# Series of extra matmuls behind the last output: a conv kernel on one core

## The chip, the cores and the metric

The kernel runs on one core of a Trainium2 chip. The metric is the device time of one execution in microseconds (us). Two runs of the kernel before gave 2524.60 and 2525.92 us, a median of 2525.26.

## The reference

An image batch `x` of shape (4, 32, 32, 16) passes through four layers, each added to its input after a group normalisation. Layers 0, 1 and 3 are of one kind, a convolution whose 3 x 3 kernel differs for each of the 1024 output positions; layer 2 works on intervals (running maxima and two small dynamic-programming steps).

```
first   = einsum('ijyx,byxc->bijc', M, inputs)
shifted = conv(inputs, G as h*w*f kernels of 3x3xC)      # for every position (i,j) an own kernel
diff    = relu(inputs[:, None, None] - shifted)
second  = einsum('ijyx,bijyxc->bijc', W, diff)
return first - second
...
x = x + conv0(_gn(x)); x = x + conv1(_gn(x)); x = x + interval2(_gn(x)); x = x + conv3(_gn(x))
```

The heavy part is `shifted`: 1024 positions x 16 filters as output rows, 144 taps and channels as the contraction, and 1024 image positions for each of 4 images as columns, in three layers. The result wanted is the final `x`.

## The kernel before

The batch is cut into two groups of two images (`NG = 2`, `GB = 2`). Three conv layers of two groups each make six phases. A phase has eight chunks (`NT`) of 128 output positions, and a chunk has 32 steps, one for each filter and image: 6 x 8 x 32 = 1536 steps.

A step computes a [128 x 1024] block: for 128 output positions, the convolution with one filter over one image, into a pair of PSUM banks (`bank_pair`, four pairs in rotation, which is all of PSUM). The upper and lower halves of the image (512 columns each) go to the two banks of the pair. The contraction is laid on 64 partitions at a time, and the array is used as two row tiles: `products` (line 601 has its matmul) issues for each of its operand pairs one matmul on partitions 0 to 63 and one on 64 to 127, which run side by side, each into its own bank. I call such two matmuls a pair. In steps with split operands there are seven pairs:

- `first_part`: two with weights `WU` and columns `iy`, two with `WL` and `iz`; then ScalarE scales the whole block in place (line 630);
- `second_part`: two with `WD` and `iyz`, one with `W9` and `im9` (the ninth tap). In this last pair one of the two matmuls has only `LAST` = 480 columns instead of `NH` = 512; which tile that is changes with the image `b`. Then VectorE takes the minimum with zero, multiplies with the weights `WT` and sums (line 646).

The operands are F32R except in the first 16 steps, which use plain f32. All is written for one `manual_schedule`: instructions stand on each engine in the order of the Python code. `conv_layer` issues the first part of a step before the second part of the step ahead of it, so that TensorE works on one step while ScalarE scales another. Preparation of weights (`prep_parts`), normalisation, the interval layer and the `first` terms are generators that are advanced between the steps. `wpool` holds the prepared weights: `parts` (both row tiles' `WU`, `WL`, `WD` for four filters) and `W9`, for a unit of four filters at a time.

At the end, the last step's second part is issued, VectorE reduces the last block and adds it to `X[1]`, and SP sends the last chunk of `X[1]` to `out`. The end of the kernel waits for all engines' queues and for the DMAs.

Of the kernel before, what the change touches and what calls it, by code (L numbers as in the profile page):

```python
# [15 lines left out]
P = 128  # L16
B, H, C = 4, 32, 16
NG = 2
GB = B // NG
# [8 lines left out]
NH = HI * H  # L28
# [3 lines left out]
FU = 4  # L32
NU = C // FU
# [9 lines left out]
def net_kernel(ctx: ExitStack, tc: tile.TileContext, x, xq, xi, convs, iv_w, iv_b, out):  # L43
# [26 lines left out]
    nc = tc.nc  # L70
# [13 lines left out]
    def bank(name):  # L84
        return bank_pair(name)[:, 0]
# [3 lines left out]
    n_chunks = len(phases) * NT  # L89
# [12 lines left out]
    raws, units, chunks = {}, {}, {}  # L102

    def load_raw(u):
        if u < n_chunks * NU:
            n = u // NU
            raws[u] = wpool.tile([P, 3, FU, P], F32, tag="raw", bufs=RAWS, name=f"raw_{u}")
            nc.sync.dma_start(raws[u], convs[phases[n // NT][1]][2][n % NT, u % NU])
# [13 lines left out]
    iy = [const.tile([P, 2, GB, NH], F32R, name=f"iy{g}") for g in range(NG)]  # L122
    iz = [const.tile([P, 2, GB, NH], F32R, name=f"iz{g}") for g in range(NG)]
    iyz = [const.tile([P, 2, GB, NH], F32R, name=f"iyz{g}") for g in range(NG)]
    im9 = [const.tile([P, GB, NH], F32R, name=f"im9{g}") for g in range(NG)]
# [45 lines left out]
    def halve(dst, src, mask):  # L171
        nc.scalar.activation(dst, src, AF.Copy, scale=mask[:, 1:2])  # L172
# [19 lines left out]
    def upper(src, n, name):  # L192

        t = work.tile([P, 2, NH], F32, tag="upper", bufs=2, name=f"upper_{name}")[:, :n]
        t = t.rearrange("p s (y x) -> p s y x", x=src.shape[3])
        nc.vector.tensor_scalar(  # L196
            t.bitcast(I32), src.bitcast(I32), HIGH, None, op0=ALU.bitwise_and
        )
        return t.rearrange("p s y x -> p s (y x)")

    def prep(u, at=0, to=FU, eng=nc.gpsimd):

        if u >= n_chunks * NU:
            return
        f0 = u % NU * FU
        for s in range(2 if u < PLAIN else 1):
            eng.tensor_tensor(  # L207
                raws[u][:, s, at:to], raws[u][:, s, at:to],
                pick[s][:, f0 + at : f0 + to].unsqueeze(2).to_broadcast([P, to - at, P]),
                ALU.subtract,  # L210
            )

    def prep_parts():

        for u in range(PLAIN, n_chunks * NU):
            parts = wpool.tile([P, 2, 3, FU, P], F32R, tag="parts", bufs=AHEAD + 1, name=f"parts_{u}")
            W9 = wpool.tile([P, FU, P], F32R, tag="W9", bufs=AHEAD + 1, name=f"W9_{u}")  # L220
            units[u] = [parts[:, :, k] for k in range(3)] + [W9]
            src = raws.pop(u)
            w8 = src[:, 0].rearrange("p f k -> p (f k)")
            WU, WL, WD = (parts[:, 0, k].rearrange("p f k -> p (f k)") for k in range(3))
            high = upper(src[:, 0:1], 1, f"w{u}")[:, 0]
            yield (IDLE,)
            halve(W9, src[:, 1], low_w)
            yield ()
            nc.scalar.activation(WD, high, AF.Copy, scale=-EPS)  # L229
            nc.gpsimd.tensor_tensor(WL, w8, high, ALU.subtract)  # L230
            nc.gpsimd.tensor_tensor(W9, W9.bitcast(F32), src[:, 2], ALU.add)  # L231
            yield ()
            nc.scalar.copy(WU, high)  # L233
            nc.gpsimd.tensor_tensor(WD, WD.bitcast(F32), WL.bitcast(F32), ALU.add)  # L234
            yield ()
            prep(u + 1)
            yield (IDLE,)
            yield (IDLE, CALM)
            for h in range(2):
                nc.sync.dma_start(  # L240
                    parts[64 * h : 64 * h + 64, 1].bitcast(F32),
                    parts[64 - 64 * h : 128 - 64 * h, 0].bitcast(F32),
                )
            load_raw(u + RAWS)
            yield (IDLE, CALM)
            yield (IDLE, CALM)
# [477 lines left out]
    pairs = const.tile([P, C // 2], F32, name="pairs")  # L724
# [17 lines left out]
    rows = const.tile([P, 2, 4], F32, name="rows")  # L742
# [23 lines left out]
    def first_stats(src, name):  # L766

        ps = bank(f"ps_{name}")
        by_batch = work.tile([P, GB], F32, tag="by_batch", name=f"by_batch_{name}")
        nc.vector.tensor_scalar_mul(by_batch, own, src)  # L770
        nc.tensor.matmul(  # L771
            ps[:, :GB], lhsT=to_rows.rearrange("p k g s -> p (k g s)"), rhs=by_batch,
            start=True, stop=True,
        )
        return ps[:, :GB]

    nc.vector.tensor_reduce(s1, XQ, axis=AX.X, op=ALU.add)
    ps = bank("ps_own")
# [3 lines left out]
    m = first_stats(s1, "m0")  # L782
# [57 lines left out]
    def rest_of_start():  # L840
# [25 lines left out]
        yield from group_norm(0, "c00", xns[0], 4)  # L866

    parts = prep_parts()
    for phase in range(len(phases)):
        conv_layer(phase, behind(phase))  # L870
    second_part(*open_steps.pop(0))
    nc.sync.dma_start(out[1][:, NT - 1], X[1][:, NT - 1])


# [74 lines left out]
```

## Time and profile before

| what | value |
|---|---|
| median of the runs | 2525.26 us |
| the profiled execution's own time | 2525.65 us |
| its span, from the first to the last instruction | 2523.9 us |
| TensorE busy, instructions | 2509.2 us, 21906 matmuls |
| VectorE, ScalarE, GpSimd busy | 2080.3, 1890.2, 1103.6 us |
| granted TensorE clock, mean over the span | 1.000 |
| last pair of matmuls starts | 2519.22 us |
| last reduction on VectorE starts, takes | 2519.71 us, 1.22 us |
| last output DMA issued, median from issue to landing | 2521.19 us, 1.4 us |

A row of the timeline has the start in us from the span's start, the time from the first start to the last end, the engine, the line, the operation, the tile written and those read, the shape, and how many instructions were merged (x4). Matmuls are pipelined: one of 512 columns is listed with 393 ns, but the next starts long before it ends, so distances between starts are what counts. Rows for weight loads (PEld) run beside those for matmuls (PE).

### The profile page before, as it was taken

How to read it: one execution, taken by the hardware profiler on the slowest of the kernel's cores; microseconds unless marked ns; L12 is line 12 of the kernel's file. 1: busy time of each engine (PE TensorE's matmuls, PEld its weight loads, DVE VectorE, ACT ScalarE, POOL GpSimd, SP SyncE). 2: the span in 40 equal slices, each digit the busy share in tenths (PEclk: the TensorE clock that was granted, in tenths of full speed). 3: DMA queues.
4: the chain of work that ended last, by engine and by line, in shares of the span. 5: the costliest groups of instructions: out<-in, count | busy, mean ns of one | idle time of the engine just before them, and what ended most of it. 6: DMA issues, size and time to landing. Idle time of an engine off the chain costs nothing.

```text
span 2523.9 us, 56662 instructions
## 1 busy us (share of the span) xinstructions
PE 2509.2 (99%) x21906; PEld 2186.7 (87%) x21906; DVE 2080.3 (82%) x3621; ACT 1890.2 (75%) x2181; POOL 1103.6 (44%) x990
## 2 busy tenths in 40 slices
PE   8999999999999999999999999999999999999999
PEld 5888888888888888888888889988999898888887
DVE  8888777888777887777788988888888887778877
ACT  3777777787777777777777777787777777777776
POOL 3445333454333335333345555454646344333332
PEclk9999999999999999999999999999999999999999
DMA  5556444464444654444454444554444466354442
GB/s 173 180 151 169 120 135 137 117 168 139 131 139 131 200 163 118 139 131 133 135 143 134 131 119 136 144 159 128 124 135 137 130 170 201 111 143 134 134 135 53
DMA packets 81182, 353.80 MB, mean 140 GB/s; under 512 B 18448, under 2 KB 20368, under 8 KB 80144
## 3 DMA queue, kind: packets, MB, share of 16 engines
q1 hardware_dynamic: 79920, 349.57, 49.2%
q8 instruction: 172, 2.82, 0.5%
q14 instruction: 98, 0.80, 0.1%
q10 hardware_dynamic: 864, 0.58, 0.1%
q0 software_dynamic: 128, 0.02, 0.0%
HBM read 199.19 MB, written 0.98 MB: 79 GB/s over the span
## 4 chain that ended last, share of the span: by engine, by line
PE 99%; ACT 0%; DVE 0%; issue 0%; POOL 0%; DVEq 0%; ACTq 0%; POOLq 0%
PE pc L601 97%; PE pf L398 1%; ACT pc L630 0%; DVE junk L646 0%; PE ps_l L521 0%; PE ps_r L534 0%; ACT L326 0%; ACT L564 0%; DVE raw L817 0%; PE ps_y L585 0%; DVE kept L761 0%; DVE kept L757 0%; PE ps_v L771 0%; DVE raw L825 0%; DVE squares L794 0%
## 5 line engine op out<-in xcount | busy, mean ns | idle before, releaser
L646 DVE SCALAR_TENSOR_TENSOR junk<-pc,WT 128x1024 f32<-128x1024 f32 x1536 | 1879.7, 1224 | 419.0 <-PE pc L601 377.7
L630 ACT ACTIVATE pc<-pc 128x1024 f32<-128x1024 f32 x1520 | 1531.8, 1008 | 599.6 <-PE pc L601 566.5
L601 PE MATMUL pc<-iy,parts 64*128 64x512 f32 x6080 | 988.7, 393 | 0.1
L601 PE MATMUL pc<-iyz,parts 64*128 64x512 f32 x6080 | 971.8, 389 | 1.9 <-ACT pc L630 1.9
L601 PE MATMUL pc<-iz,parts 64*128 64x512 f32 x6080 | 968.3, 387 | 0.0
L601 PEld LDWEIGHTS pc<-iz,parts 64*128 64x128 f32 x6080 | 624.3, 184 | 85.7
L601 PEld LDWEIGHTS pc<-iyz,parts 64*128 64x128 f32 x6080 | 611.9, 184 | 89.1 <-ACT pc L630 5.8
L230 POOL TENSOR_TENSOR parts<-raw,upper_w 128x512 fp32r<-128x512 f32 x190 | 247.3, 1301 | 1008.6 <-PE pc L601 847.4
L601 PEld LDWEIGHTS pc<-iy,parts 64*128 64x128 f32 x6080 | 619.6, 184 | 78.2 <-issue 4.4
L601 PE MATMUL pc<-im,W 64*128 64x480 f32 (+1 forms) x3072 | 623.4, 384 | 0.0
L601 PEld LDWEIGHTS pc<-im,W 64*128 64x128 f32 x3072 | 311.4, 185 | 46.3 <-issue 3.4
L231 POOL TENSOR_TENSOR W<-W,raw 128x512 fp32r<-128x512 f32 x190 | 248.5, 1308 | 1.9 <-ACT W L172 1.6
L234 POOL TENSOR_TENSOR parts<-parts 128x512 fp32r<-128x512 f32 x190 | 247.8, 1304 | 2.7 <-ACT parts L229 2.5
L207 POOL TENSOR_TENSOR raw<-raw,ident 128x512 f32<-128x512 f32 x190 | 201.5, 1061 | 42.8 <-DMA raw<-in_g 34.8
L172 ACT ACTIVATE W<-raw,low_w 128x512 fp32r<-128x512 f32 x190 | 135.9, 715 | 0.1
L646 DVE DVE_READ_ACCUMULATOR junk<-pc,WT 128x1 f32 x1536 | 127.5, 83 | 0.0
L229 ACT ACTIVATE parts<-upper_w 128x512 fp32r<-128x512 f32 x190 | 118.5, 624 | 4.7 <-DVE upper_w L196 4.7
L233 ACT CAST parts<-upper_w 128x512 fp32r<-128x512 f32 x190 | 117.0, 616 | 0.0
L661 POOL TENSOR_SCALAR acc<-acc 128x32 f32<-128x32 f32 x40 | 11.5, 289 | 163.3 <-DVE junk L646 158.9
L196 DVE TENSOR_SCALAR upper_w<-raw 128x512 int32<-128x512 int32 x190 | 82.4, 433 | 0.2
L553 POOL TENSOR_TENSOR tables<-ft_b,rt 128x1089 f32<-128x1089 f32 x16 | 37.6, 2351 | 0.2
L553 POOL TENSOR_TENSOR tables<-ft_a,rt 128x1089 f32<-128x1089 f32 x16 | 37.7, 2355 | 0.0
(138 smaller groups left out, 397.3 us busy)
## 6 DMA issues: line engine op xcount, KB each, us to landing
raw<-in_g SPq DMA_DIRECT2D x190, 768.0 KB, 7.0
parts<-parts SPq DMA_DIRECT2D x380, 384.0 KB, 5.0
WT<-in_w SPq DMA_DIRECT2D x48, 512.0 KB, 4.7
MT<-in_mt SPq DMA_DIRECT2D x6, 2048.0 KB, 13.6
raw<-xs SPq DMA_DIRECT2D x120, 67.8 KB, 2.4
raw<-in_xi SPq DMA_DIRECT2D x3, 271.0 KB, 4.5
raw<-in_xi SPq DMA_DIRECT2D x1, 813.0 KB, 6.8
xs<-xt SPq DMA_DIRECT2D x20, 34.0 KB, 2.0
```

Of the source, the lines that this page charges most:

```text
L172: nc.scalar.activation(dst, src, AF.Copy, scale=mask[:, 1:2])
L196: nc.vector.tensor_scalar(t.bitcast(I32), src.bitcast(I32), HIGH, None, op0=ALU.bitwise_and)
L207: eng.tensor_tensor(raws[u][:, s, at:to], raws[u][:, s, at:to], pick[s][:, f0 + at : f0 + to].unsqueeze(2).to_broadcast([P, to - at, P]), ...
L229: nc.scalar.activation(WD, high, AF.Copy, scale=-EPS)
L230: nc.gpsimd.tensor_tensor(WL, w8, high, ALU.subtract)
L231: nc.gpsimd.tensor_tensor(W9, W9.bitcast(F32), src[:, 2], ALU.add)
L233: nc.scalar.copy(WU, high)
L234: nc.gpsimd.tensor_tensor(WD, WD.bitcast(F32), WL.bitcast(F32), ALU.add)
L553: nc.gpsimd.tensor_tensor(t, ft[:, i, :].unsqueeze(1).to_broadcast([P, T1, T1]), rt, ALU.add,)
L601: nc.tensor.matmul(ps[:, half, :n], lhsT=w[r], rhs=v[r] if n == NH else v[r][:, :n], start=first and k == 0, stop=k == len(pairs) - 1, ski ...
L630: nc.scalar.activation(ps, ps, AF.Copy, scale=1.0 + EPS)
L646: nc.vector.scalar_tensor_tensor(junk, ps.rearrange("p h n -> p (h n)"), 0.0, chunks[n], op0=ALU.min, op1=ALU.mult, accum_out=accs[phase][ ...
```

## The change

Behind the last output's DMA in the code, TensorE gets further matmuls, whose results stay in PSUM and are read by nobody. `more` writes one series: 20 times a matmul on each of the two row tiles (or on tile 0 alone, with 64 or with 128 rows), with weights that change each time. Its arguments set the number of columns `n`, where the columns start (`xo`), where the result starts (`po`), and whether one matmul of `lead` columns on tile 0 goes ahead. `replay` repeats the matmuls of the last unit's eight steps (four filters, two images), both parts in one go with no scaling and no reduction between; `cuts` gives some of the seven pairs fewer columns, on both tiles. The line `all_parts[0] = parts` keeps the last weights for that.

```
+    all_parts = [None]
...
             units[u] = [parts[:, :, k] for k in range(3)] + [W9]
+            all_parts[0] = parts
...
     second_part(*open_steps.pop(0))
     nc.sync.dma_start(out[1][:, NT - 1], X[1][:, NT - 1])
 
+    xf = iy[0].rearrange("p s b n -> p (s b n)")
+    wf = all_parts[0].rearrange("p a k f n -> p (a k f n)")
+    last_unit = units[n_chunks * NU - 1]
...
+    def more(name, n=NH, xo=0, wo=0, po=0, tiles=(0, 1), rows=64, lead=0, count=20):
+        ps = bank_pair(f"more_{name}_")
+        if lead:
+            nc.tensor.matmul(ps[:, 0, :lead], lhsT=wf[:64, :P], rhs=xf[:64, :lead], start=True, stop=True)
+        for k in range(count):
+            x0 = k % 2 * 512 + xo
+            w0 = k % 20 * 128 + wo
+            for h in tiles:
+                r = slice(64 * h, 64 * h + rows)
+                nc.tensor.matmul(
+                    ps[:, h, po : po + n], lhsT=wf[r, w0 : w0 + P], rhs=xf[r, x0 : x0 + n],
+                    start=True, stop=True,
+                )
+
+    def replay(name, cuts):
+        pair = [bank_pair(f"more_{name}{b}_") for b in range(GB)]
+        WU, WL, WD, W9 = last_unit
+        for f in range(FU):
+            for b in range(GB):
+                pairs = (
+                    [(WU[:, s, f], iy[1][:, s, b]) for s in range(2)]
+                    + [(WL[:, s, f], iz[1][:, s, b]) for s in range(2)]
+                    + [(WD[:, s, f], iyz[1][:, s, b]) for s in range(2)]
+                    + [(W9[:, f], im9[1][:, b])]
+                )
+                for k, (w, v) in enumerate(pairs):
+                    n, xo, po = cuts.get(k, (NH, 0, 0))
+                    for h in range(2):
+                        r = slice(64 * h, 64 * h + 64)
+                        nc.tensor.matmul(
+                            pair[b][:, h ^ b, po : po + n], lhsT=w[r], rhs=v[r][:, xo : xo + n],
+                            start=k == 0, stop=k == len(pairs) - 1, skip_group_check=True,
+                        )
+
+    more("a")
+    more("b", n=496)
+    more("c", n=480)
+    more("d", n=464)
+    more("e", n=496, po=16)
+    more("f", n=496, po=16, xo=16)
+    more("g", tiles=(0,))
+    more("h", tiles=(0,), rows=P)
+    more("i", xo=128)
+    more("j", xo=256)
+    more("k", lead=128)
+    more("l", lead=200)
+    more("m", lead=256)
+    more("n", lead=320)
+    more("o", lead=400)
+    more("p", n=384)
+    replay("q", {})
+    replay("r", {6: (496, 0, 0)})
+    replay("s", {6: (480, 0, 0)})
+    replay("t", {1: (496, 0, 16), 3: (496, 0, 0), 6: (496, 0, 0)})
+    replay("u", {1: (496, 16, 16), 6: (496, 0, 0)})
+    replay("v", {1: (480, 0, 32), 3: (480, 0, 0), 6: (480, 0, 0)})
+    replay("w", {1: (496, 0, 0), 2: (496, 0, 16), 3: (496, 0, 0)})
```

## The prediction

> **What bounds the kernel now.** I read the profile in this order: busy shares, slices, the chain that ended last, the costliest groups, and then the timeline of the last 14 us, because everything that is added stands behind the last real matmul.
>
> The page says TensorE:
>
> ```profile
> PE 2509.2 (99%) x21906; PEld 2186.7 (87%) x21906; DVE 2080.3 (82%) x3621; ACT 1890.2 (75%) x2181; POOL 1103.6 (44%) x990
> ...
> PEclk9999999999999999999999999999999999999999
> ...
> PE 99%; ACT 0%; DVE 0%; issue 0%; POOL 0%; DVEq 0%; ACTq 0%; POOLq 0%
> ```
>
> The reader is to see that TensorE is busy throughout at its full granted clock, and that the chain that ended last runs on it for 99% of the span. Work put into its queue has nothing to hide behind, except after its own last instruction. The groups give the shapes that recur in the change:
>
> ```profile
> L601 PE MATMUL pc<-iy,parts 64*128 64x512 f32 x6080 | 988.7, 393 | 0.1
> L601 PE MATMUL pc<-im,W 64*128 64x480 f32 (+1 forms) x3072 | 623.4, 384 | 0.0
> L601 PEld LDWEIGHTS pc<-iy,parts 64*128 64x128 f32 x6080 | 619.6, 184 | 78.2 <-issue 4.4
> ```
>
> The 393 ns of one matmul is not its price: matmuls are pipelined and run in pairs, one on each row tile. The price is the distance between starts, which the TensorE timeline near the end shows:
>
> ```profile
> 2510.04 0.63 PE L601 MATMUL pc<-iy,parts 64*128 64x512 f32 x4
> 2510.51 0.62 PE L601 MATMUL pc<-iz,parts 64*128 64x512 f32 x4
> 2510.97 0.63 PE L601 MATMUL pc<-iyz,parts 64*128 64x512 f32 x4
> 2511.42 0.40 PE L601 MATMUL pc<-im,W 64*128 64x480 f32 x2
> 2511.63 0.66 PE L601 MATMUL pc<-iy,parts 64*128 64x512 f32 x4
> ...
> 2516.45 0.63 PE L601 MATMUL pc<-iy,parts 64*128 64x512 f32 x4
> ...
> 2518.65 0.73 PE L601 MATMUL pc<-iyz,parts 64*128 64x512 f32 x4 [0.41 <-ACT pc L630]
> 2519.22 0.40 PE L601 MATMUL pc<-im,W 64*128 64x480 f32 x2
> ```
>
> An x4 row is two pairs, the x2 row one. From 2510.04 to 2516.45 four steps of seven pairs pass: 6.41 us for 28 pairs, 229 ns a pair. Two of the 28 passes on each tile are 480 columns long (the short half changes tile with the batch). What a column is worth, the groups kept apart by shape tell: im matmuls of 512 columns have a mean of 391 ns, those of 480 have 377, so 32 columns are 14 ns, 0.44 ns each, and 512 are 224. If the short passes' saving is kept, a full pair costs (6410 + 2 x 14) / 28 = 229.9 ns; if it is lost, 228.9. I take **230 ns for a pair of 512 columns**. Single stretches of these lines bound it: two iy pairs take 0.47 us (235 each), the im pair 0.21 to 0.22 (its 512-column half no more than 222).
>
> **The change, part by part.** It removes nothing. In the order of the program's instructions, SP, ScalarE, VectorE and GpSimd issue what they issued before (466, 2187, 1969 and 971 rows in both), no DMA is added, and TensorE's queue gets its new work after the last real matmul. `all_parts[0] = parts` and the flattened views are bookkeeping without instructions.
>
> Counted from the code: 14 series of 20 pairs and two (g, h) of 20 single matmuls, with five extra lead matmuls: 14 x 40 + 2 x 20 + 5 = 605. A replay is 4 filters x 2 batches x 7 pairs = 56 pairs; seven of them have 392 pairs, 784 matmuls. In all **1389 matmuls, each with its weight load, in 712 time slots** (280 pairs and 40 singles in the series, 392 pairs in the replays) and five leads.
>
> 1. Slots at full width: 712 x 0.230 = 163.8 us. A single of g or h is priced as a pair: the two tiles run side by side, so leaving one out frees no time on the other. No row shows a stream on one tile alone, or 512 columns over 128 rows. Its ends are 224 ns, the columns alone, and 330, if no weight load is covered: at 2518.65, after the wait for ScalarE, the first pair has to wait for its weights, and the row's 0.73 us are 0.10 more than the usual 0.63. So 40 slots are worth from -0.2 to +4.0 us against 230; I stay at 230, the row of the same 64x512 shape.
> 2. Fewer columns. In the series: 3 x 20 x 16 (b, e, f) + 20 x 32 (c) + 20 x 48 (d) + 20 x 128 (p) = 5120. In the replays 8 steps each: r 16, s 32, t 48, u 32, v 96, w 48 columns a step, 272 x 8 = 2176. At 0.44 ns a column that is 2.2 + 1.0 = **-3.2 us** if all of it is kept, nothing if something other than columns sets the pace. Both tiles are shortened alike, so neither holds back the other; the im pair's 0.21 to 0.22 against 0.23 says that even a single short half gives something back. I take -3.2.
> 3. Leads: 128 + 200 + 256 + 320 + 400 = 1304 columns, 0.57 us, and five times the 6 ns by which a 230 ns slot exceeds its 224 ns of columns: **+0.6 us**. The second tile's first matmul stands behind the first tile's in the queue, so a lead is paid once and not regained; at worst each costs a slot, 1.15 us.
> 4. Waits. PSUM has four bank pairs. Series a to d wait for VectorE's reads of the last four real ones. The last ends at 2520.9 (the chain's reduction of 1.24 us from 2519.71), and d, which needs it, is due 13 us after the real matmuls. Later series and replays wait for TensorE's own work two or more allocations back, over 4 us old. I cost them at nothing; if a satisfied wait costs the 0.04 us that the chain shows as issue after ScalarE's work, 30 of them make 1.2 us.
> 5. The tail that was exposed becomes cover. After the last real pair (2519.22) the old span had the last reduction, the output DMA (issued at 2521.19, landing 1.4 us later, so at 2522.6) and 1.3 us of closing. The new stream starts one slot later, at 2519.45, and the output lands under it. The end is then TensorE's last result, 0.16 us (393 - 230) after its slot, and about 1.1 us of closing (0.9 to 1.3: the closing behind the DMA, or its part after the queues' waits).
>
> Added TensorE time: 163.8 - 3.2 + 0.6 = **161.2 us**. New span: 2519.45 + 161.2 + 0.16 + 1.1 = 2681.9, against 2523.9: +158.0. The profiled execution's own time is 2525.65, 1.75 outside the span, so 2683.7 by its clock; it is 0.4 above the runs' median of 2525.26, so against the median **2683.3**, a ratio of 1.063.
>
> On one point a rule speaks against this. The row: a pair comes every 230 ns, though 512 columns take 224 and a weight load alone is listed with 184; so a tile's load runs while the same tile still computes. The Trainium skill, "TensorE: Matmul & The Clock Gate", section "The mechanism" of its Part 3, says that a weight load overlaps running matmuls only when the row group differs. An estimate by its section "LDWEIGHTS (loading the stationary operand)", 128 columns at 1.2 per ns, would put 107 ns beside every slot's columns, some 70 us more. The trace denies it for pairs; for the one-tile series g and h no row decides, and there the rule would add about 4 us.
>
> **Rivals.**
>
> - *Short passes save nothing and one-bank streams run at the slow rows.* All passes of a series write one bank pair, like the iy rows at 235, where the real step changes banks twice. Then 712 x 5 ns = +3.6, and +3.2 for lost savings: up to 2690. For it: a slot exceeds its columns by 6 ns, so something besides columns is in it. Against it: iyz, whose two pairs and im share a bank pair, takes 0.45 to 0.47 for two, so one bank alone isn't slow.
> - *Passes run faster when VectorE and ScalarE are idle.* At 222 a slot: -5.7 us, 2678. For it: no TensorE row exists without the others at work. Against it: the steps from 2510 to 2516 differ little in length although the other engines come and go within each.
> - *One-tile and 128-row series lose their overlap or need several sweeps.* The 330 ns bound adds 4.0: 2687.3. The plain f32 matmuls of the first steps (638 ns as listed, against 393) show that a type can cost more; h at four times 230 would add 13.8 us: 2697.
> - *The work isn't there.* The results are unused; if what builds the program leaves them out, the time stays at 2525.3, no change. It decides only if nearly all of it goes: 161 us must shrink below 52 for the time to stay within 2%. Against it: the kernel's `spare` activations feed nothing, and the trace has them (L326 x8, L564 x4), and `junk` is written 1536 times and never read.
>
> **How the numbers follow.** Forecast, 2680 to 2687: 0.70. Slow rows and lost savings, 2687 to 2690: 0.12. Faster passes, 2677 to 2680: 0.10. One-tile or 128-row costs, 2687 to 2697: 0.05. Work left out: 0.02. Something else: 0.01. The range of 2677 to 2692 takes in the bounds of the slot's price (222 to 235 ns), of the savings and of the one-tile series; it leaves out h in several sweeps. 2% of this kernel, 50 us, is about what a measurement can tell from no change. All cases but the last two are 6% slower: slower 0.97, same 0.02, faster 0.01.
>
> **What would show it.** TensorE's busy time up by some 161 us to about 2670, with 21906 + 1389 = 23295 matmuls, all new ones after 2519; the granted clock full to about 2681, where the window after 2520 now has 0.69; no idle time at series starts. Starts in series a 230 ns apart, in b, e, f 223, in c 216, in d 209, in p 174; a replay q of 12.9 us, v of 12.6. Wrong would be series b to f as long as a (step 2), g at another pace than a (step 1), a gap before each series (step 4), or an output that lands after the new matmuls (step 5).

## The result, and the profile after

The changed kernel takes 2683.07 us in the median of two runs (2682.70 to 2683.44), against 2525.26 before: a ratio of 1.0624, 95% interval 1.0599 to 1.0650. The forecast was 2683.3. The profiled execution took 2682.70, its span is 2681.0.

The busy shares, the granted clock in 40 slices and the chain that ended last, of the changed kernel:

```profile
PE 2669.6 (100%) x23295; PEld 2366.0 (88%) x23295; DVE 2080.7 (78%) x3621; ACT 1890.5 (71%) x2181; POOL 1103.5 (41%) x990
...
PEclk9999999999999999999999999999999999999999
...
PE 99%; ACT 0%; DVE 0%; issue 0%; POOL 0%; ACTq 0%; DVEq 0%; POOLq 0%
```

TensorE has the 1389 matmuls more, is busy 160.4 us longer, and keeps its clock; the other engines do what they did. The TensorE timeline from the last real matmuls on (start, time from the first start to the last end, line, tile written and tiles read, shape, count):

```profile
2518.39 0.73 PE L604 MATMUL pc<-iyz,parts 64*128 64x512 f32 x4 [0.41 <-ACT pc L633]
2518.96 0.40 PE L604 MATMUL pc<-im,W 64*128 64x480 f32 x2
2519.18 4.72 PE L894 MATMUL more_a__31840<-iy,parts 64*128 64x512 f32 x40
2523.74 4.56 PE L894 MATMUL more_b__31881<-iy,parts 64*128 64x496 f32 x40
2528.14 4.50 PE L894 MATMUL more_c__31922<-iy,parts 64*128 64x480 f32 x40
2532.47 4.36 PE L894 MATMUL more_d__31963<-iy,parts 64*128 64x464 f32 x40
2536.67 4.56 PE L894 MATMUL more_e__32004<-iy,parts 64*128 64x496 f32 x40
2541.07 4.70 PE L894 MATMUL more_f__32045<-iy,parts 64*128 64x496 f32 x40
2545.61 4.70 PE L894 MATMUL more_g__32086<-iy,parts 64*128 64x512 f32 x20
2550.24 4.83 PE L894 MATMUL more_h__32107<-iy,parts 128*128 128x512 f32 x20
2555.00 4.85 PE L894 MATMUL more_i__32128<-iy,parts 64*128 64x512 f32 x40
2559.68 4.70 PE L894 MATMUL more_j__32169<-iy,parts 64*128 64x512 f32 x40
2564.22 0.22 PE L888 MATMUL more_k__32210<-iy,parts 64*128 64x128 f32 x1
2564.22 4.83 PE L894 MATMUL more_k__32210<-iy,parts 64*128 64x512 f32 x40
```

The first column is the one to subtract. No gap stands between series: b begins 4.56 us after a, c 4.40 after b. The last matmul starts at 2679.64. With a slot of 0.23 behind it the added stream is 160.7 us long, 71.6 of it series (to 2590.78) and 89.1 replays; the forecast's parts were 71.95 and 89.2. The span ends 1.13 us after the last slot, forecast 1.26.

So the added stream holds to half a microsecond. But its rows don't: b, c and d take 220, 217 and 210 ns a slot where 223, 216 and 209 were expected, e stands at 220 and f, with as many columns, at 227. Replay q takes 12.75 us where 12.9 was expected. A series at full width that is left alone (j) needs 4.54 us, 227 ns a slot and not 230. Something in the real steps made their slots longer, and something in the short passes gives back less than their columns. That was what the runs had to settle.

### The profile page after: what moved, and what is told of

Read it like the earlier page. It is cut to its first block, busy times and chain, and to the rows that moved or that the text cites. A ratio compares the mean times of both kernels' runs of the same rounds, so it can differ in the third digit from the quotient of the medians.

```text
span 2681.0 us, 59440 instructions
## 1 busy us (share of the span) xinstructions
PE 2669.6 (100%) x23295; PEld 2366.0 (88%) x23295; DVE 2080.7 (78%) x3621; ACT 1890.5 (71%) x2181; POOL 1103.5 (41%) x990
## 4 chain that ended last, share of the span: by engine, by line
PE 99%; ACT 0%; DVE 0%; issue 0%; POOL 0%; ACTq 0%; DVEq 0%; POOLq 0%
PE pc L604 92%; PE pf L401 1%; ACT pc L633 0%; PE more_q__32461 L914 0%; PE more_s__32690 L914 0%; PE more_u__32918 L914 0%; PE more_u__32917 L914 0%; PE more_w__33146 L914 0%; PE more_s__32689 L914 0%; PE more_q__32462 L914 0%; PE more_r__32575 L914 0%; PE more_r__32576 L914 0%; PE more_t__32804 L914 0%; PE more_v__33032 L914 0%; PE more_t__32803 L914 0%
## 5 line engine op out<-in xcount | busy, mean ns | idle before, releaser
L604 PE MATMUL pc<-iyz,parts 64*128 64x512 f32 x6080 | 981.8, 389 | 1.9 <-ACT pc L633 1.9
L604 PE MATMUL pc<-iz,parts 64*128 64x512 f32 x6080 | 978.5, 387 | 0.0
L604 PEld LDWEIGHTS pc<-iz,parts 64*128 64x128 f32 x6080 | 638.7, 184 | 76.3
L604 PEld LDWEIGHTS pc<-iyz,parts 64*128 64x128 f32 x6080 | 624.0, 184 | 82.0 <-ACT pc L633 5.8
L604 PEld LDWEIGHTS pc<-iy,parts 64*128 64x128 f32 x6080 | 631.9, 184 | 70.7 <-issue 4.4
L604 PE MATMUL pc<-im,W 64*128 64x480 f32 (+1 forms) x3072 | 633.1, 384 | 0.0
L604 PEld LDWEIGHTS pc<-im,W 64*128 64x128 f32 x3072 | 321.4, 185 | 41.9 <-issue 3.3
```

Of the source, the lines that this page charges most:

```text
L604: nc.tensor.matmul(ps[:, half, :n], lhsT=w[r], rhs=v[r] if n == NH else v[r][:, :n], start=first and k == 0, stop=k == len(pairs) - 1, ski ...
```

## The experiments

Theory A: a stream of matmuls has a settled pace, at which its slots no longer change (227 ns at 512 columns), and a pass of some other lengths disturbs it, so that the following slots are longer; the real steps carry such a pass (480 columns) in each step. Theory B: the price is a constant and the columns, as in the prediction. Theory C: the real steps' excess over the replays comes from the other engines' traffic.

**All passes at full width, and 496 columns in place of 480.** Both are the kernel before, without the added series:

```
-LAST = (HI - 1) * H
+LAST = NH           # e1_full
+LAST = NH - 16      # e2_496
```

The added columns multiply the zero padding beside the image, so the sums are the same.

> All passes have 512 columns; the added series are absent. Theory A (pacing): in replay q, with every pass at 512, a step takes 1587 ns (226.7 a slot), in the real steps with one short half 1604, so the short pass upsets the slots behind it; without it about 1520 steps gain 17 ns each: 2525 - 26 = 2499. Theory B (columns set the price, as the prediction took it): each step loses the 14 ns of one half on one tile, 7 ns a step: 2536. Theory C (the real steps' excess over the replay comes from the other engines' traffic): 2525, no change.

> The short half of the last pass has 496 columns in place of 480; the added series are absent. Theory A: 496-column passes in replay r stood at 220 ns and left the slots behind them at 226.7, so a step takes 1587 - 3.3 = 1584: 2525 - 31 = 2494. Theory B: half of 7 ns more a step than with 480, 2530. Theory C: 2525.

Measured: 2503.25 us with all at 512 (ratio 0.9914, interval 0.9897 to 0.9930), and 2498.77 with 496 (0.9898, 0.9883 to 0.9912), against 2525.02 in the same session. More columns, less time: B and C fall, the sign and nearly the size of A hold (21.8 and 26.3 us of the 26 and 31 expected). Six real steps of the kernel with 512, TensorE's timeline, the iy rows alone and the last:

```profile
2484.40 0.62 PE L601 MATMUL pc<-iy,parts 64*128 64x512 f32 x4
...
2485.99 0.62 PE L601 MATMUL pc<-iy,parts 64*128 64x512 f32 x4
...
2493.92 0.62 PE L601 MATMUL pc<-iy,parts 64*128 64x512 f32 x4
```

and of the kernel with 496:

```profile
2479.88 0.62 PE L601 MATMUL pc<-iy,parts 64*128 64x512 f32 x4
2480.33 0.62 PE L601 MATMUL pc<-iz,parts 64*128 64x512 f32 x4
2480.79 0.62 PE L601 MATMUL pc<-iyz,parts 64*128 64x512 f32 x4
...
2489.38 0.62 PE L601 MATMUL pc<-iy,parts 64*128 64x512 f32 x4
```

Six steps take 9.52 us (1587 ns each) and 9.50 (1583), against 1602 in the kernel before (6.41 us for four), with ScalarE and VectorE reading PSUM all the while: the settled pace is reached beside their work. The x4 rows of these steps are all 0.62 long, where before they came as 0.62 to 0.66. This is also the version that beats both kernels: one constant, 26 us.

Of the 4 to 5 us that are missing from the expectation, about 2 come from the step of the kernel before, which takes 1602 ns and not 1604. The rest was not traced further. In both kernels the chain has other work for 3% (`PE 97%; DVE 1%; DMA 1%`), where it was 1% before.

**Which last pass disturbs.** Replayed steps behind the last output of the kernel before, 24 a variant; only the last pass of the seven, and as in the real steps only on one tile, alternating, is short:

```
+                for k, (w, v) in enumerate(pairs):
+                    for h in range(2):
+                        n = last if k == 6 and (both or h ^ b) else NH
...
+    for last in (512, 508, 504, 500, 496, 492, 488, 484, 480):
+        steps(f"kick{last}", last)
+    steps("both480", 480, True)
+    steps("both496", 496, True)
```

> Before, with replayed steps behind the last output, 24 steps each, the last pass short on one tile alone and alternating with the image as in the real steps, from 512 down by 4 to 480; then both tiles short by 32 and by 16. Theory A: 1587 ns a step at 512, about 1584 at 496, about 1604 at 480 as in the real steps, 1606 with both at 480 and 1580 with both at 496. Theory B: an even fall from 1587 to 1580 at 480 on one tile, 1573 on both.

First matmuls of some variants, from narrow windows of TensorE's timeline (512, 508, 504, 500; then 496, 492):

```profile
2518.15 0.64 PE L935 MATMUL more_kick__31840<-iy,parts 64*128 64x512 f32 x4
...
2556.24 0.41 PE L935 MATMUL more_kick__32178<-iy,parts 64*128 64x512 f32 x2
...
2594.47 0.42 PE L935 MATMUL more_kick__32516<-iy,parts 64*128 64x512 f32 x2
...
2633.07 0.39 PE L935 MATMUL more_kick__32854<-iy,parts 64*128 64x512 f32 x1
...
2671.42 0.43 PE L935 MATMUL more_kick__33192<-iy,parts 64*128 64x512 f32 x2
...
2709.44 0.41 PE L935 MATMUL more_kick__33530<-iy,parts 64*128 64x512 f32 x2
```

The distance to the next first start, divided by 24, is the step (the others from the same view):

| columns of the short half | 512 | 508 | 504 | 500 | 496 | 492 | 488 | 484 | 480 | both tiles 480 |
|---|---|---|---|---|---|---|---|---|---|---|
| ns a step | 1587 | 1593 | 1608 | 1598 | 1584 | 1589 | 1602 | 1591 | 1602 | 1603 |

With both tiles at 496 the single starts of the last 16 steps give 1580. A holds within 3 ns at each value it named, where B expected an even fall. With 480 columns the replay, which has no other engine beside it, takes the 1602 ns of the real step. Of these lengths 496 alone is better than 512. Why 496 leaves the pace alone and the others do not is open.

**One stream or two.** Series of 60 slots with every twentieth pass short, on both tiles, on one tile of 64 rows, and on 128 rows:

```
+            m = n if k % 20 == 10 else 512
...
+    for n in (512, 496, 480, 448, 384, 256):
+        pulse(f"two{n}", n, (0, 1), 64)
...
+        pulse(f"one{n}", n, (0,), 64)
...
+        pulse(f"full{n}", n, (0,), P)
```

> Before with series of 60 slots in which every twentieth pass is short (512, 496, 480, 448, 384 or 256 columns), once on both tiles, once on one tile of 64 rows, once on 128 rows. If each stream's own weight loads and passes lose step after a short pass, all three kinds show the same: 496 saves its 7 ns and nothing follows, 480 saves 10 to 13 ns and the next five to ten slots stand at 228 to 236, 15 to 35 ns in sum. If the two tiles disturb each other, the one-tile and the 128-row series settle at once behind a short pass.

TensorE's timeline, the six series on one tile (512, 496, 480, 448, 384, 256):

```profile
2600.36 13.76 PE L926 MATMUL more_one__32566<-iy,parts 64*128 64x512 f32 x60
2613.96 13.74 PE L926 MATMUL more_one__32627<-iy,parts 64*128 64x512 f32 x60
2627.54 13.86 PE L926 MATMUL more_one__32688<-iy,parts 64*128 64x512 f32 x60
2641.24 13.74 PE L926 MATMUL more_one__32749<-iy,parts 64*128 64x512 f32 x60
2654.82 13.68 PE L926 MATMUL more_one__32810<-iy,parts 64*128 64x512 f32 x60
2668.34 13.50 PE L926 MATMUL more_one__32871<-iy,parts 64*128 64x512 f32 x60
```

13.60 us without short passes, 13.58 with three of 496 columns, and 13.70 with three of 480: each 480 pass makes the series 33 ns longer, instead of 13 ns shorter. The starts of single matmuls in the trace give the course: 227, 227, 213 (the short one), then 235, 233, 236, 224, 231, 236, 228, 233, 231, 226, 227. The same numbers stand in the series on both tiles and on 128 rows, to the nanosecond or two. So the disturbance is a matter of one stream of weight loads and passes, not of the tiles against each other. The slots behind a 480 pass lose 47 ns in sum, more than the 15 to 35 expected. Passes of 448 and 384 columns disturb too (at 448: 199, then 236, 228, 232, 231, 227), but save enough: 7 and 27 ns net.

**What a column is worth when the stream is settled**, and singles:

```
+    for n in (512, 504, 496, 488, 480, 472, 464, 448, 432, 416, 384, 320, 256, 512):
+        more(f"law{n}", n=n, count=40)
+    more("one", tiles=(0,), count=60)
+    more("full", tiles=(0,), rows=P, count=60)
```

> Before, with other series behind the last output: 40 pairs each of 512 down to 256 columns, then 60 single matmuls on one tile of 64 rows, then 60 on 128 rows. Theory A: settled slots of 226.7, 220.0, 216.7 and 210.0 ns at 512, 496, 480 and 464 as in the changed kernel, and 504, 488, 472 stand near the next longer multiple of 16 columns; singles settle at 226.7 on one tile and on 128 rows. Theory B: a straight line, 0.44 ns a column below 230. If a tile's weight load did not run beside its own matmul, singles would take about 330.

The last 384, 320 and 256 columns, 512 again, and the singles (TensorE's timeline):

```profile
2603.70 7.12 PE L894 MATMUL more_law__32650<-iy,parts 64*128 64x384 f32 x80
2610.64 6.04 PE L894 MATMUL more_law__32731<-iy,parts 64*128 64x320 f32 x80
2616.50 4.98 PE L894 MATMUL more_law__32812<-iy,parts 64*128 64x256 f32 x80
2621.29 9.28 PE L894 MATMUL more_law__32893<-iy,parts 64*128 64x512 f32 x80
2630.39 13.76 PE L894 MATMUL more_one__32974<-iy,parts 64*128 64x512 f32 x60
2644.08 13.89 PE L894 MATMUL more_full__33035<-iy,parts 128*128 128x512 f32 x60
```

| columns | 512 | 504 | 496 | 488 | 480 | 472 | 464 | 448 | 432 | 416 | 384 | 320 | 256 |
|---|---|---|---|---|---|---|---|---|---|---|---|---|---|
| ns a slot, last 20 | 226.6 | 226.6 | 223.4 | 220.0 | 216.6 | 213.4 | 208.8 | 202.6 | 195.8 | 186.7 | 173.3 | 146.6 | 120.0 |

From 512 to 256 columns the slot falls by 106.6 ns, 0.416 a column, with about 13 ns that don't depend on them; between, some lengths stand up to 3.4 ns above that line. A's guess of steps of 16 columns is not what the table shows, and 496 settled at 223 here though at 220 in series b, with the same operands: a stream can settle at more than one pace. Singles take 226.6 ns too, on one tile and on 128 rows.

**Every added pass at full width.** The changed kernel without short passes, offsets and leads:

```
-    more("b", n=496)
+    more("b")
...
-    replay("v", {1: (480, 0, 32), 3: (480, 0, 0), 6: (480, 0, 0)})
+    replay("v", {})
```

> The changed kernel with every added pass at 512 columns, no offsets and no leads; one tile in g and 128 rows in h stay. Settled slots: 712 x 226.7 = 161.4 us and about 0.5 for the starts of g, h and i, 161.9 against 160.7 in the changed kernel, so 2683.1 + 1.2 = 2684.3, and 1587 ns for every replayed step. The prediction's columns: short passes saved 3.2 and leads cost 0.6, so 2.6 more than the changed kernel, 2685.7.

Measured 2683.98 us (2682.96 to 2684.46), ratio to before 1.0625, 1.0609 to 1.0641; 0.9 above the changed kernel's median, with overlapping runs. The traces separate them better: from the first added start to the last 161.66 us against 160.47. All the offsets, cuts and leads together are worth 1.2 us; A expected 1.2, the prediction's columns 2.6. In replays r to v the short passes make it plain (first starts in the changed kernel, from narrow windows of TensorE's timeline; s cuts one pass to 480, u starts one at element 16):

```profile
2603.53 0.39 PE L914 MATMUL more_r__32575<-iy,parts 64*128 64x512 f32 x1
...
2616.17 0.39 PE L914 MATMUL more_s__32689<-iy,parts 64*128 64x512 f32 x1
...
2628.97 0.39 PE L914 MATMUL more_t__32803<-iy,parts 64*128 64x512 f32 x1
...
2641.57 0.39 PE L914 MATMUL more_u__32917<-iy,parts 64*128 64x512 f32 x1
...
2654.35 0.39 PE L914 MATMUL more_v__33031<-iy,parts 64*128 64x512 f32 x1
...
2666.93 0.39 PE L914 MATMUL more_w__33145<-iy,parts 64*128 64x512 f32 x1
```

r, s, t, u and v take 12.64, 12.80, 12.60, 12.78 and 12.58 us; at full width each takes 12.69. Two of the five are longer with fewer columns: s by its 480 passes, while u also starts a pass at element 16, which costs time by itself (below). The five together save less than 0.1 us where their columns were priced at 0.8.

The leads can be read too. In the changed kernel, around the end of series o:

```profile
2586.98 0.61 PE L894 MATMUL more_o__32378<-iy,parts 64*128 64x512 f32 x3
2587.23 0.51 PE L894 MATMUL more_p__32420<-iy,parts 64*128 64x384 f32 x2
2587.44 0.39 PE L894 MATMUL more_o__32378<-iy,parts 64*128 64x512 f32 x1
```

and in the kernel at full width:

```profile
2565.03 4.70 PE L894 MATMUL more_k__32210<-iy,parts 64*128 64x512 f32 x40
...
2587.69 4.70 PE L894 MATMUL more_p__32415<-iy,parts 64*128 64x512 f32 x40
```

Without leads, k to o take 22.66 us. With them the first pass of p starts 23.01 us after k's lead, 0.35 more, and the last pass of o starts only 0.21 behind it: the two tiles no longer run in step. At the end of the stream one tile is still 0.36 us behind the other (the last two im passes start at 2679.28 and 2679.64). Together the leads cost about 0.7 us.

**The tail as cover.** The kernel before with 12 pairs behind the last output:

```
+    more("a", count=12)
```

> Before with one series of 12 pairs of 512 columns behind the last output. The prediction's fifth step: 12 x 0.227 = 2.7 us end at 2521.9 and the output's landing at about 2522.6 still sets the end, no change: 2525.0. If the tail covers nothing: 2527.7.

Measured 2525.31 us against 2526.36 in the same session, ratio 0.9997, 0.9987 to 1.0007. In its timeline stands

```profile
2519.40 2.91 PE L894 MATMUL more_a__31840<-iy,parts 64*128 64x512 f32 x24
```

The output lands 1.4 us after its issue at 2521.16, and the span is the 2523.9 of the kernel before. 12 pairs are free.

**Where the columns are read from.** Long series of 512, 496 and 480 columns with different starts:

```
+    for xo in (0, 4, 8, 16, 32, 48):
+        addr(f"n512x{xo}", 512, xo)
...
+    for po in (4, 16, 32):
+        addr(f"n480p{po}", 480, 0, po)
+    addr("n480same", 480, turn=False)
+    addr("n480old", 480, new=False)
```

> Before with series of 40 pairs behind the last output: 512, 496 and 480 columns that start 0, 4, 8, 16, 32 or 48 elements into the operand; 480 with the result moved by 4, 16 and 32; 480 and 512 with one operand or one weight block repeated. If the place that the columns are read from sets the surplus (as series f, 496 from element 16, at 227 against 220 for b and e suggests), 496 stands at 227 for 16 and 48 and at 220 for 0 and 32, 512 rises above 227 for starts that are not multiples of 32, and the place of the result does nothing. If the length alone sets it, all starts show 227, 220 and 217. If the weight loads do, repeating one weight block changes the slot.

| start, elements | 0 | 4 | 8 | 16 | 32 | 48 |
|---|---|---|---|---|---|---|
| 512 columns, ns a slot, last 20 | 226.6 | 231.7 | 233.4 | 229.0 | 232.6 | 233.3 |
| 496 columns | 223.4 | 223.4 | 224.5 | 226.6 | 226.6 | 220.0 |
| 480 columns | 216.6 | 216.7 | 220.0 | 218.4 | 220.0 | 216.0 |

The place of the result, a repeated operand and a repeated weight block change nothing (216.6 and 216.7). The start does, but by none of the three rules expected: multiples of 32 are not the quick ones. At 512 columns every start from 4 to 48 is slower than 0, which stood at 226.6 to 226.7 in each run, and series i and j settle at 227 from 128 and 256. At 496 and 480 the table shows less: each start was run once, in one order, and 496 from element 0 has settled at 223.4 and, in series b and e, at 220, so what ran before may be part of these differences. Why the start matters is open. It wasn't tried whether other data types behave so.

## Why the prediction was right, and where it was not

The bound was read rightly: the work stands on TensorE's queue behind everything else, and its slots are the time. That the total came out within 0.3 us of the median is luck: errors of up to 2.4 us in its terms nearly cancelled, and the two runs are 0.7 us apart. Against the profiled execution the sum was 0.9 us too high (a span of 2681.9 forecast, 2681.0 measured): 0.5 in the stream, 0.3 in where it starts (2519.18 for 2519.45), 0.1 in the closing.

- **Step 1, the slot.** 230 ns was the mean of the real steps, which carry a 480-column pass. Undisturbed it is 226.7: 712 slots are 161.4 us, 2.4 less than priced. The prediction took the short half's saving as kept, and so put the other passes at 230; the runs with 512 and 496 show that the short half itself made them longer than they would be without it. The bounds of 222 and 235 were the two sides of one disturbed course, not two kinds of pass.
- **Singles.** One tile alone and 128 rows settle at 226.6 ns, the same as a pair, as step 1 took it. What was not priced are the changes between 64 and 128 rows: g, h and i need 4.63, 4.76 and 4.68 us where j needs 4.54; with a's unsettled start that is 0.5 us. From g's last matmul to h's first pass 315 ns, and h's first slot is 337 ns: each about 0.1 longer than a settled one, and from h to i it is the same (319 and 332). h's first weight load comes late:

```profile
2550.24 0.53 PEld L894 LDWEIGHTS more_h__32107<-iy,parts 128*128 128x128 f32 x3 [0.35 <-issue]
```

g's last matmul starts at 2549.92, so this load starts 0.31 us behind it, where within g the next load starts 4 ns behind a matmul. The Trainium skill, "TensorEngine Tiling (Array Packing)", section "Key Properties", says that a change of tiling mode drains TensorE; the late load agrees, though the trace does not name what it waited for.
- **Step 2, the short passes.** -3.2 was priced. Against the kernel at full width, cuts and leads together give 1.2; with the leads at 0.7, the cuts gave 1.9. This is the mis-sized term. The series, where all passes are alike, gave 1.8 of the 2.2 priced (f, which starts at element 16, gave none); the replays, where short passes stand among long ones, gave about 0.1 of 1.0. The price of a column was right (0.44 taken, 0.416 settled), but short passes among long ones cost the slots behind them.
- **Step 3, the leads.** 0.6 was priced and about 0.7 paid. The way was another: k's lead and a 512-column pass both start at 2564.22, so the second tile's first pass did not wait for the lead; the first tile paid for it and fell behind the second.
- **Step 4, the waits.** Nothing, as taken: no idle time stands at a start of a series.
- **Step 5, the tail.** Confirmed by the 12 free pairs.

In sum: -2.4 for the slot, +1.4 for short passes and leads together, +0.5 for the changes of tiling are -0.5, the distance between the priced 161.2 and the 160.7 of the trace.

Of the rivals, *short passes save nothing* had the right suspicion (something besides columns is in a slot, and in the replays short passes did save next to nothing) with the wrong cause, one PSUM bank, and the wrong sign for the slots. *Faster when the other engines are idle* named a pace near the settled one, but the kernel with 512 reaches 1587 ns a step with VectorE and ScalarE at work, so idleness isn't the cause. *One-tile series lose their overlap* falls at 226.6 ns, and with it, for this case, the rule weighed there, that a weight load runs beside matmuls of another row group only. *The work isn't there* falls at 23295 matmuls.

## What to carry to other kernels

The mean distance of instructions in a loop is not the price of one: look at the single distances, and where they vary in a fixed pattern, ask which pass starts the pattern. Cutting a few columns off one pass among equal ones can cost more than it saves; try a length beside it (here 496 for 480, 26 us of 2525) and no cut at all. When a total fits to 0.01%, check its terms anyway: here three were off by 0.5 to 2.4 us and nearly cancelled.

## What the runs showed of the hardware

- A stream of weight load and matmul pairs keeps 226.7 ns for 512 columns of F32R, whether on two tiles of 64 rows, one, or 128 rows, and reaches 120.0 ns at 256 columns with new weights each time.
- One pass of 480 columns among 512 makes about nine following slots 224 to 236 ns long, 33 ns lost net; one of 496 loses nothing and saves 7.
- Starting 512 columns at element 4 to 48 of the operand costs 2 to 7 ns a slot; starting at 128 or 256 (series i and j) costs nothing.
- The two tiles' streams are loosely coupled: starts do not keep the order of the program between them. After the leads, a 512-column pass of a later series starts ahead of the last pass of the series before and of its own series' lead (line 888), which stand before it in the code, as these rows of the changed kernel's TensorE timeline show:

```profile
2573.29 0.40 PE L894 MATMUL more_m__32294<-iy,parts 64*128 64x512 f32 x1
2573.34 0.39 PE L894 MATMUL more_l__32252<-iy,parts 64*128 64x512 f32 x1
...
2573.56 0.27 PE L888 MATMUL more_m__32294<-iy,parts 64*128 64x256 f32 x1
```

The trace does not name the tile; by the code the lead is on the first tile, so the early pass is taken to be the second's. The Trainium skill, "TensorE: Matmul & The Clock Gate", section "The mechanism", calls matmuls strictly ordered in start and end; these starts are not, by 0.05 and 0.27 us.
